# A three-layer feature-interaction network on one core: a new order of the set-up, folded weights made on TensorE, pooling inside the last chunk

## The chip, the cores and the metric

One core of a Trainium2 chip. The time is the device time of a whole run in microseconds (us); medians of several runs are given, with the lowest and highest where it matters. Positions in a trace are us from the start of the profiled span.

## The reference, cut to what matters

```python
# x: 1024 samples, F = 64 fields, E = 16 (1024, 64, 16); W0, W1, W2: 128 x 4096; fc_w: 1 x 256
h = x
for i in range(3):
    z = einsum('bfe,bge->bfge', x, h)              # all products of fields
    y = einsum('oc,bce->boe', W[i], z) + b[i]      # 128 outputs
    if i < 2:
        x_i, h = y[:, :64], y[:, 64:]              # one half is pooled, the other goes on
    else:
        x_i = y
    xs.append(x_i)
out = concat(xs, axis=1).sum(axis=2) @ fc_w.T + fc_b   # 1024 x 1
```

Only a weighted sum of the pooled outputs is wanted, so fc can be multiplied into the weights ahead of time. With V0, V1, V2 = fc times the pooled rows of W0, W1, W2 (each 64 x 64), layers 1 and 2 become sums of h1 times something that is linear in products of x again: M = V2 folded into the lower half of W1 (64 x 64 x 64), and M1 = the contraction of M with the same products of x that give h1. So one pass over the products yields h1 (64 columns) and M1 (64 columns) side by side, 128 columns of weights in all.

## The kernel before: the parts that matter

The samples run in 32 chunks of 32 (512 columns). A chunk has four VectorE products of 128 x 2048 (four tiles of 512 each), 16 matmuls over them, and one more over a "diagonal" tile. The weights are `w_all`, 17 tiles of 128 columns: 0 to 63 for h1 (from W0), 64 to 127 for M1. M must be read skewed, so it is stored to DRAM and read back: the **detour**. M1 of the first chunk can't begin until it is over.

```python
# V2 on VectorE: W2 is weighed with fc and summed, four times, ahead of everything
def weigh(w, fc, out):
    nk, n = out.shape[-1], fc.shape[-1]
    w = w.rearrange("p (k c) -> p k c", c=n)
    nc.vector.tensor_tensor(w, w, fc.unsqueeze(1).to_broadcast([128, nk, n]), ALU.mult)
    nc.vector.tensor_reduce(out, w, AX.X, ALU.add)

for k in range(4):
    cols = slice(k % 2 * 1024, (k % 2 + 1) * 1024)
    weigh(w2s[k // 2][:, cols], fcr[:, 128:256], v2h[:, 8 * k : 8 * k + 8])
# ... v2h into v2t, then M: eight matmuls, copies to m_sb, and the stores
nc.scalar.dma_start(out=md[0:64, 0:32, :], in_=m_lo)
nc.sync.dma_start(out=md[0:64, 32:64, :], in_=m_hi)
nc.scalar.dma_start(out=md[0:64, 64:96, :], in_=m_lo)
nc.sync.dma_start(out=md[64:96, 32:64, :], in_=m_hi[0:32])
nc.scalar.dma_start(out=md[64:96, 0:32, :], in_=m_lo[0:32])
nc.sync.dma_start(out=md[64:96, 64:68, :], in_=m_lo[0:32, 0:4, :])
nc.sync.dma_start(out=md[64:68, 64:96, :], in_=m_lo[0:4])     # corner, overlaps the last
# ...
side_by_side(ph, 0, range(NT + 1))        # h1 of chunk 0, in two halves of the array
# ... ten skewed reads of md, V1's and V0's loads, chunk 1's load
nc.vector.tensor_tensor(w_all[:, 0:NT, 64:128], ms1, ms2, ALU.add)
side_by_side(pq, 1, range(NT))            # M1 of chunk 0
weigh(w1x, fcr[:, 64:128], v1h)           # V1; V0 likewise, inside chunk 2
for c in range(1, NCH + 1):               # ... full chunks, 128 columns
    ...
# pooling behind the last chunk: 2 x 4 matmuls over acc, two activations, the output
```

## Time and profile before

| Part of the span | from (us) | to | length |
|---|---|---|---|
| V2 on VectorE, until M's matmuls start | 0 | 17.26 | 17.3 |
| M's matmuls and copies | 17.26 | 23.98 | 6.7 |
| stores of M | 23.98 | 36.2 | 12.2 |
| skewed reads, addition | 36.2 | 46.10 | 9.9 |
| M1 of chunk 0 to the last full-width matmul | 46.10 | 527.66 | 481.6 |
| behind it | 527.66 | 536.1 | 8.4 |

The median of the first three runs was 539.54 us (538.16 to 539.59). The chain of waits, the costliest groups and three stretches are shown in the prediction. Here is the timeline's line for the start of M1 (start, length, engine, line, operation, and the idle time ahead of it with what ended it):

```profile
46.10 8.42 PE L239 MATMUL pq<-z,w_all 128*64 128x256 f32 x64 [9.14 <-DVE w_all L280]
```

TensorE had been idle for 9.14 us when the addition that completes M1's weights released it.

### The profile page before, as it was taken

The numbers are of one execution on the slowest core, as the hardware profiler recorded it, in microseconds if no ns is written. First come the engines' busy times: TensorE is split into PE (matmuls) and PEld (weight loads), VectorE is DVE, ScalarE is ACT, GpSimd is POOL, SyncE is SP. The second block draws the span as 40 slices with busy tenths as digits, with TensorE's granted clock in tenths as the row PEclk, the third lists the DMA queues.
The fourth block names the chain that finished last, engine by engine and source line by source line (L and its number), as shares of the span: only waits on it lengthen the run. The fifth ranks groups of instructions, "written<-read, shape, count | busy, mean of one in ns | idle before, by whom it ended". The sixth has DMA issues, their size and how long they took to land.

```text
span 536.1 us, 3189 instructions
## 1 busy us (share of the span) xinstructions
PE 496.6 (93%) x1262; PEld 222.0 (41%) x1262; DVE 362.1 (68%) x222; ACT 79.1 (15%) x135; POOL 5.7 (1%) x18
## 2 busy tenths in 40 slices
PE   0465996999999999999999999999999999999997
PEld 0243442444444444444444444444444444444442
DVE  4654968687776767687776767687776767677822
ACT  0010110011111111011111111011111111101111
POOL 4000000000000000000000000000000000000000
PEclk9987998999999999999999999999999999999999
DMA  8669924433241434343341434434341424430000
GB/s 280 232 176 352 378 90 157 156 156 158 103 160 59 159 147 156 156 158 156 107 171 46 167 137 156 156 158 156 123 167 51 166 120 156 158 156 0 0 1 0
DMA packets 14152, 77.00 MB, mean 144 GB/s; under 512 B 3861, under 2 KB 4533, under 8 KB 5302
## 3 DMA queue, kind: packets, MB, share of 16 engines
q1 hardware_dynamic: 12058, 74.82, 36.2%
q10 hardware_dynamic: 1792, 1.98, 1.5%
q8 instruction: 10, 0.16, 0.1%
q0 software_dynamic: 288, 0.00, 0.0%
q14 instruction: 4, 0.03, 0.0%
HBM read 74.63 MB, written 2.17 MB: 143 GB/s over the span
## 4 chain that ended last, share of the span: by engine, by line
PE 89%; DMA 6%; DVE 3%; issue 0%; ACTq 0%; SPq 0%; ACT 0%; DVEq 0%
PE acc L191 80%; PE acc L205 5%; PE y L222 2%; DMA md<-m_sb 2%; DMA xb<-in_xrb 2%; DMA fcr<-in_fc_w 1%; PE pm L153 1%; DVE v2h L133 1%; DVE w L132 1%; DMA ms<-md 1%; DVE z L182 1%; PE po L354 0%; DVE uu L226 0%; DVE acc L227 0%; ACTq L271 0%
## 5 line engine op out<-in xcount | busy, mean ns | idle before, releaser
L191 PE MATMUL acc<-z,w_all 128*128 128x512 f32 x992 | 432.8, 594 | 4.7 <-DVE z L182 4.7
L191 PEld LDWEIGHTS acc<-z,w_all 128*128 128x128 f32 x992 | 188.9, 191 | 243.4 <-issue 230.0
L182 DVE TENSOR_TENSOR z<-xa,xb 128x2048 f32<-128x2048 f32 x128 | 284.5, 2281 | 1.6 <-DMA xb<-in_xrb 1.5
L214 DVE SCALAR_TENSOR_TENSOR uu<-acc,bh,q 64x512 f32<-64x512 f32 x31 | 23.1, 744 | 138.0 <-ACT q L213 138.0
L213 ACT COPY q<-acc 64x512 f32<-64x512 f32 x31 | 18.0, 582 | 398.6 <-PE acc L205 398.6
L205 PE MATMUL acc<-zl,w_all 128*128 128x512 f32 x62 | 31.7, 592 | 0.0
L153 PE MATMUL pm<-w1s,v2t 64*64 64x512 f32 x16 | 5.9, 863 | 17.3 <-DVE v2t L143 17.3
L196 ACT ACTIVATE zl<-xa 64x512 f32<-64x512 f32 x32 | 20.1, 629 | 5.6 <-DVE w_all L170 5.2
L227 DVE TENSOR_REDUCE acc<-uu 128x64 f32<-128x1024 f32 x16 | 19.5, 1220 | 0.5
L197 ACT COPY zl<-xa 64x512 f32<-64x512 f32 x32 | 19.7, 615 | 0.4
L201 ACT COPY xx<-xa 64x512 f32<-64x512 f32 x32 | 19.6, 614 | 0.4
L205 PEld LDWEIGHTS acc<-zl,w_all 128*128 128x128 f32 x62 | 11.8, 190 | 14.8 <-issue 14.8
L239 PE MATMUL pq<-z,w_all 128*64 128x256 f32 x64 | 8.4, 429 | 9.1 <-DVE w_all L280 9.1
L222 PE MATMUL y<-xx,bd 128*128 128x512 f32 x32 | 16.3, 592 | 0.0
L226 DVE SCALAR_TENSOR_TENSOR uu<-y,cx,xx 128x512 f32<-128x512 f32 x16 | 12.0, 751 | 4.8 <-PE y L222 4.3
L239 PE MATMUL ph<-z,w_all 128*64 128x256 f32 x64 | 8.8, 444 | 4.5 <-DVE w_all L170 4.5
L153 PEld LDWEIGHTS pm<-w1s,v2t 64*64 64x64 f32 x16 | 2.9, 196 | 19.4 <-DVE v2t L143 17.3
L239 PEld LDWEIGHTS pq<-z,w_all 128*64 128x64 f32 x64 | 5.0, 157 | 12.5 <-DVE w_all L280 9.6
L132 DVE TENSOR_TENSOR w<-w,fcr 128x1024 f32<-128x1024 f32 x4 | 4.9, 1217 | 7.2 <-DMA fcr<-in_fc_w 7.2
L222 PEld LDWEIGHTS y<-xx,bd 128*128 128x128 f32 x32 | 6.1, 190 | 7.7 <-issue 7.7
L239 PEld LDWEIGHTS ph<-z,w_all 128*64 128x64 f32 x64 | 5.3, 160 | 8.5 <-DVE w_all L170 5.4
L279 DVE MEMSET ms<- 64x64 f32 x1 | 0.1, 112 | 7.5 <-DMA ms<-md 7.5
(46 smaller groups left out, 39.2 us busy)
## 6 DMA issues: line engine op xcount, KB each, us to landing
xa<-in_xra SPq DMA_DIRECT2D x32, 1024.0 KB, 4.8
xb<-in_xrb SPq DMA_DIRECT2D x32, 1024.0 KB, 6.9
w<-in_wv SPq DMA_DIRECT2D x4, 512.0 KB, 7.3
w1s<-in_w1h SPq DMA_DIRECT2D x1, 1024.0 KB, 10.4
md<-m_sb ACTq DMA_DIRECT2D x2, 512.0 KB, 7.0
w1x<-in_wx SPq DMA_DIRECT2D x1, 1024.0 KB
w0x<-in_wx SPq DMA_DIRECT2D x1, 1024.0 KB, 12.5
w0t<-in_w0a SPq DMA_DIRECT2D x1, 544.0 KB
```

The costliest lines, as they stand in the source:

```text
L153: nc.tensor.matmul(pm[to], v2t[to], w1s[to, cols], start=True, stop=True)
L182: nc.vector.tensor_tensor(z, xas[c], xbs[c][:, j, :].unsqueeze(1).to_broadcast([128, NI, N]), ALU.mult)
L191: nc.tensor.matmul(accs[c], w_all[:, t, :], z[:, i, :], start=(t == 0), stop=False)
L196: nc.scalar.activation(zl[0:64], xas[c][0:64, 0, :], AF.Square)
L197: nc.scalar.copy(zl[64:128], xas[c][64:128, 0, :])
L201: nc.scalar.copy(xxs[c // 2][to], xas[c][to, 0, :])
L205: nc.tensor.matmul(accs[c], w_all[:, NT, :], zls[c], start=False, stop=True)
L213: nc.scalar.copy(q, accs[c][64:128])
L214: nc.vector.scalar_tensor_tensor(uus[c // 2][to, 0, :], accs[c][0:64], bh1[0:64], q, ALU.add, ALU.mult)
L222: nc.tensor.matmul(ys[k], bd, xxs[k], start=True, stop=True)
L227: nc.vector.tensor_reduce(acc[:, :, k, :], uus[k].rearrange("p k (b e) -> p k b e", e=E), AX.X, ALU.add)
L239: nc.tensor.matmul(p[halves[n]], w_all[:, t, cols], z[:, n * H2 : (n + 1) * H2], start=(t == 0), stop=(t == NT),)
```

## The change

Its intent: TensorE should have work while M makes its detour, and V0 to V2 should not cost VectorE's time. Loads of x and W0 come first; the h1 halves of three chunks (not one) run ahead of M1; V2 and later V0, V1 are made by TensorE, with fc as a weight of 32 equal columns in four quarters of the array, and spread by small SBUF-to-SBUF DMAs; 15 of the 16 pairs of chunks are pooled inside the last chunk.

```diff
+    x_tiles(0)
+    load_xa(0)
+    load_xb(0, slice(0, 1))                                # x first, xb and W0 in pieces
+    nc.sync.dma_start(out=w0s[:, 0:NI], in_=w0p[:, 0:NI])
+    load_xb(0, slice(1, NJ))
+    nc.sync.dma_start(out=w0s[:, NI:NT], in_=w0p[:, NI:NT])
+    for k in range(2):
+        nc.sync.dma_start(out=w2s[k], in_=wv2[:, k * 2048 : (k + 1) * 2048])
+    nc.sync.dma_start(out=w1s, in_=w1h)
+    load_chunk(1)
     ...
+    product(0, 0)
+    h1_weights(slice(0, NI))
+    side_by_side(0, 0, group(0))
     ...                                                    # groups 1, 2 likewise
+    load_chunk(2)
-    for k in range(4):
-        weigh(w2s[k // 2][:, cols], fcr[:, 128:256], v2h[:, 8 * k : 8 * k + 8])
+    for n in range(2):
+        pv = ps.tile([128, 512], F32, tag="set", name=f"pv2_{n}")
+        for k in range(4):
+            nc.tensor.matmul(pv[32 * k : 32 * k + 32], fv2, w2s[n][:, k * 512 : (k + 1) * 512],
+                             start=True, stop=True, tile_position=(0, 32 * k))
+        nc.scalar.copy(v2r[:, n, :], pv)
+        for to in halves:
+            nc.scalar.dma_start(out=v2t[to.start + 32 * n : to.start + 32 * n + 32],
+                                in_=v2r[0:128:32, n, :].rearrange("k (o f) -> k o f", f=F))
     ...                                                    # M's matmuls; four copies on ScalarE
-    nc.sync.dma_start(out=md[0:64, 32:64, :], in_=m_hi)
-    nc.scalar.dma_start(out=md[0:64, 64:96, :], in_=m_lo)
+    nc.scalar.dma_start(out=md[0:64, 32:64, :], in_=m_hi)
+    nc.sync.dma_start(out=md[0:64, 64:96, :], in_=m_lo)
-    nc.sync.dma_start(out=md[64:68, 64:96, :], in_=m_lo[0:4])
+    nc.sync.dma_start(out=md[64:68, 68:96, :], in_=m_lo[0:4, 4:32, :])
+    for c in (1, 2):                                       # h1 of chunks 1, 2 in the detour
+        last_tile(c)
+        for j in range(NJ):
+            product(c, j)
+            side_by_side(c, 0, group(j))
+        side_by_side(c, 0, [NT])
     ...                                                    # reads, addition
+    for k in range(2):                                     # the upper rows of W0, W1
+        nc.sync.dma_start(out=w01s[k], in_=w01[:, k * 2048 : (k + 1) * 2048])
     ...                                                    # V0, V1 as V2; M1 of chunks 0 to 2
+            if c == NCH - 1:
+                pool(first, 1)                             # 15 pairs, inside the last chunk
+                pool(first, 0)
```

(`for c in (1, 2)` stands for two written-out blocks.)

## The prediction

> **What bounds the kernel now.** I read the page's rows by busy time first, then the chain of waits, then stretches of the first 90 us and the order of events in them. The costliest groups (busy us, mean ns of one, idle before):
>
> ```profile
> L191 PE MATMUL acc<-z,w_all 128*128 128x512 f32 x992 | 432.8, 594 | 4.7 <-DVE z L182 4.7
> L182 DVE TENSOR_TENSOR z<-xa,xb 128x2048 f32<-128x2048 f32 x128 | 284.5, 2281 | 1.6 <-DMA xb<-in_xrb 1.5
> ```
>
> 31 of the 32 chunks use 16 tiles each and each fp32 matmul leaves two records: 31 x 16 x 2 = 992. TensorE is busy 93% of the span, VectorE 68%. The chain, in order of time (start, us, what):
>
> ```profile
> 0.75 6.40 DMA fcr<-in_fc_w
> ...
> 17.26 5.93 PE pm L153 x16
> ...
> 25.17 8.63 DMA md<-m_sb
> ...
> 33.86 2.33 DMA md<-m_sb
> ...
> 37.81 4.62 DMA ms<-md
> ...
> 83.89 2.29 DVE z L182
> ...
> 107.93 13.73 PE acc L191 x32
> 121.66 0.86 PE acc L205 x2
> ...
> 527.69 0.59 ACT q L213
> ...
> 531.14 1.90 PE po L354 x8
> ```
>
> From 107.93 on a chunk costs 13.73 + 0.86 = 14.59 us with no gap, so 0.858 us for one matmul of 512 columns, plus 0.86 for V0x once in a pair of chunks. VectorE needs 4 x 2.28 + 0.74 + (0.75 + 1.22)/2 = 10.9 us a chunk and follows. The steady part can't shrink; only what surrounds it can: about 56 us ahead of the first full chunk, a hole near 82 to 86, and 8.4 us behind the last V0x matmul. Stretches (PE, PEld, DVE, ACT, POOL busy, then clock, DMA share, GB/s):
>
> ```profile
> 38.00:40.00 2.00, 0.00 (x0) 0.00 (x0) 0.00 (x0) 0.00 (x0) 0.00 (x0) 1.00 1.01 246
> 82.00:84.00 2.00, 0.00 (x0) 0.00 (x0) 1.97 (x3) 0.00 (x0) 0.00 (x0) 1.00 0.02 4
> 86.00:88.00 2.00, 1.78 (x2) 0.79 (x3) 2.00 (x2) 0.00 (x0) 0.00 (x0) 0.58 0.46 127
> ```
>
> TensorE has nothing to do while M travels to memory and back, and nothing at 82, where VectorE weighs W0 ahead of the products; after the hole the clock is 0.58.
>
> **What the Trainium skill says.** "TensorE: Matmul & The Clock Gate", Part 1: after an idle window of about 3.4 us the array falls to half clock and needs a busy window to recover. The trace agrees: TensorE idled 4.5 us before the first h1 contraction, whose clock was 0.57 in 28 to 30 us and 1.00 from 32 on. "TensorEngine Tiling (Array Packing)", Key Properties: tiles of the array work independently. It agrees for two column halves: M1's 16 tiles (64 records of 256 columns) took 8.42 us from cold; alone they would need 64 x 0.215 = 13.8 us at full clock, side by side 6.85. Four quarters appear in no row yet. "DMA: Bandwidth & Descriptors", Queues, rings and completion order: an engine takes turns between queues by packet, so a small transfer still waits behind a full queue. The 16 KB copy of M's diagonal took 5.3 us to land beside the chunk loads, which agrees.
>
> **The change part by part.**
>
> 1. *Start.* V2 first (four weighings and sums on VectorE, 17.26 us until M's matmuls could start) becomes x and W0 first. Needed for the first product: 1 MB xa + 0.25 MB xb; then 0.25 MB of W0. Data starts to flow at about 2 us; the stretches read 37 to 199 GB/s until 6 us, when the broadcast read of fc (128 rows of the same 1 KB, landed 7.15) ends, and 383 to 434 GB/s from then on. I take that coincidence as the cause, and the change drops that read, so I reckon with 0.41 MB/us from 2.0: x at 5.1, W0's piece at 5.8. Product 5.4 to 7.7, weights 0.3 (a quarter of 1.23), TensorE starts at 8.0. Four tiles cold at 2 x 0.427 = 0.853 us: 11.4. Rest of W0 added (three quarters of 1.23 = 0.92) by 11.4, third product at 13.8, so three groups are through at about 15.7.
> 2. *V2 on TensorE.* Two rounds of four matmuls in quarters, 0.86 us a round if they run together: 1.7 us, to 17.5 (W2 has landed: 5 MB, 14.2). Then ScalarE in order: copy 0.59, two DMA issues at about 0.55, copy 0.59, two issues: the last is issued at about 19.7. Landing beside a full load queue 4.5 to 5.3 (rows above): v2t at 24.5. This takes the place of VectorE's 17.26: M's matmuls start 7 us later than before.
> 3. *M.* Group 3 and the diagonal end at 19.5; TensorE idles 5 us and is cold, so M's 16 records cost 5.9 as before: 30.3. ScalarE's last copy 0.6. The stores took from 23.98 to 34.35 (the third on ScalarE's queue, issued 25.85 + 8.5 landing) and then the overlapping corner 2.33 more; the change cuts the overlap, so 10.4: 41.3. The skewed reads took 8.6 (36.2 to 44.8), the addition 1.23: M1 can begin at **51.2**, against 46.1.
> 4. *Filling the detour.* Chunks 1 and 2's h1 halves, 2 x 17 x 0.43 = 14.6 us of TensorE, run between 30 and 46. VectorE makes their 8 products from 21.5 (8 MB landed) to about 40, so they are in time. About 5 us stay idle, and the restart is cold.
> 5. *From M1 on, on TensorE alone:* cold restart 1.6 (8.42 - 6.85); M1 of three chunks 3 x 6.85 = 20.6; three diagonals 1.3; V0 and V1 1.7; constants 0.45; 29 chunks x 14.59 = 423.1; 16 V0x x 0.858 = 13.7; pooling of 15 pairs inside the last chunk, two matmuls of 480 columns, 2 x 0.80 = 1.6. Sum 464.1. Before, the same stretch is 527.66 - 46.10 = 481.6. The gain of 17.5 is the two h1 halves (14.6) and the hole at 82 with its cold restart (4.3 + about 2), less V0/V1 and pooling.
> 6. *Tail.* Behind the last matmul: q 0.59, factors 0.74, a sum of 64x512 (half of 1.22, 0.65), a matmul of 32 columns about 0.3, activation 0.25 (its 1x1 row), the output 2.35 (533.75 to 536.1), joints 0.2: 5.1, against 8.4.
>
> Sum: 51.2 + 464.1 + 5.1 = 520.4 us of span. The timed median lies 3.4 above the span of the profile before, its own profiled run 1.9 above; with 2.3 between them I predict **522.7 us**, 16.8 less, 3.1%.
>
> **Rivals.**
>
> (a) *V2's way through SBUF is short.* If the DMAs land in about 2.5 us, v2t is there at 22, TensorE idles under 3 us, stays at full clock and M's matmuls cost 3.5, not 5.9. M1 begins near 46.5: measured about 518. For it: the loads are in another queue and these pieces are 8 KB each. Against: no small transfer under load landed below 3 us in the trace before.
>
> (b) *The slow start stays*, because it belongs to the first microseconds of any run and not to the broadcast read. Then 1.25 MB is there only at 7.4, all of step 1 to 3 slips by 2.3, and the time is 525. For it: those packets of W2 moved slowly on their own queue; a later load (86.2) had no slow ramp, which speaks against.
>
> (c) *The four quarters run one after another.* V2 costs 6.9 instead of 1.7, and V0/V1 the same: 10 us, so 533, within 2%. Against: two halves did run together, and nothing ties the quarters. I give it 7%.
>
> (d) *VectorE or a buffer becomes the bound.* W01's second MB, chunks 3 and 4 queue behind the addition of M1, 5 MB: chunk 3 at 9.5 us after M1 begins, its products by 18.7, chunk 4's by 28, factors and V0x's product by 31. TensorE wants chunk 3 at 26.5, the next V0x at 33.4, chunk 4 at 41. The margins are 7.8, 2.7 and 13 us, so no stall, but the 2.7 is thin and worth at most a few us. With 13 product buffers later, VectorE's 10.9 against 14.59 leaves it ahead. V0 and V1's six DMAs must land while M1 of chunk 2 (6.85 us) runs: two copies, six issues, landing makes 7.5; a wait of 0 to 2 us.
>
> (e) *The gain is hidden anyway.* The share of busy time says no: TensorE is on the chain for 89% of the span, and each us taken from its stream shifts all behind it.
>
> **Range and chances.** Steps 5 and 6 rest on durations of the trace and may be off by 2 us together; the start of M1 carries the doubt, 46.5 to 54. That spans 517 to 526; stalls of (d) and measuring scatter widen it upward, so 516.5 to 529.5. The threshold for faster by 2% is 528.7, 6 us above my number: it takes (b) with stalls, or (c), to miss it. Chance of faster 0.85, same 0.14, slower 0.01.
>
> **What would show each step.** Start: the first h1 matmul near 8.0 (10.3 if the slow start stays), and DMA above 350 GB/s from 3 us. V2: its eight matmuls (16 records) in 1.7 to 2 us, 7 if they are serial. M's matmuls start at 24.5, 5.9 long and cold, with an idle TensorE of some 5 us ahead. M1 begins at 51, after an idle stretch of 5 us, not 9. From there no gap of TensorE above 1 us to the end, which comes 5.1 behind its last full matmul. I am wrong if TensorE waits for VectorE in chunks 3 to 5, if the second detour (V0, V1) stops it ahead of the diagonals, or if the steady chunk is no longer 14.59 us.

## The result, and the profile after

| | median (us) | lowest to highest | runs |
|---|---|---|---|
| before | 539.32 | 538.16 to 539.59 | 4 |
| after | 535.58 | 535.20 to 535.99 | 4 |

The ratio of after to before is 0.9935 (95% interval 0.9918 to 0.9952): faster by 0.65%, within 2%, and 12.9 us above the 522.7 predicted. Ratios here and below are the recorded ones, for the runs of the same rounds; they are not quite the ratios of the medians quoted. The profiled run of after took 535.20 us with a span of 533.4 at a mean granted clock of 0.982; before's took 537.95, 536.1 and 0.987.

The chain of waits of after, in order of time (start, us, what), answers to the chain in the prediction:

```profile
2.12 9.51 DMA xb<-in_xrb
...
15.18 5.67 PE acc L224 x32
20.85 1.04 PE pv L273 x8
...
22.53 1.12 ACTq L280
...
25.47 6.13 DMA v2t<-v2r
31.61 6.03 PE pm L296 x16
...
41.34 8.93 DMA md<-m_sb
...
51.70 4.56 DMA ms<-md
...
56.28 5.17 DMA ms<-md
...
61.84 1.24 DVE w_all L341
...
63.12 15.96 PE acc L224 x128
...
528.68 0.59 ACT q L194
...
530.82 0.23 PE po L402 x2
```

Up to 63.12 the chain is made of transfers, VectorE and a few short pieces of TensorE: M's way. From there it is TensorE without a gap. M1 begins at 63.12, where before had 46.10. That alone is 17.0 us lost. What was won lies behind it: from M1's start to the last full-width matmul 528.66 - 63.12 = 465.5 us against 481.6, a gain of 16.0; behind the last matmul 533.4 - 528.66 = 4.7 against 8.4, a gain of 3.7. 16.0 + 3.7 - 17.0 = 2.7, the difference of the two spans.

TensorE's waits in after (engine and line, what ended the wait: us in total, times, longest) name the same places:

```profile
PE acc L224 <- DVE w_all L245: 11.5, 2, 10.1
PE acc L224 <- DVE w_all L341: 10.7, 1, 10.7
PE pm L296 <- DMA v2t<-v2r: 6.6, 1, 6.6
```

The first is the start, the second the wait for M1's weights, the third the wait for V2's scatter. There is no wait for VectorE's products behind M1 and none for V0 and V1. The first two costly groups by busy time show why the rest went well (busy us, mean ns of one, idle before):

```profile
L167 PE MATMUL acc<-z,w_all 128*128 128x512 f32 x928 | 405.5, 592 | 0.0
L224 PE MATMUL acc<-z,w_all 128*64 128x256 f32 x384 | 48.6, 416 | 22.2 <-DVE w_all L245 11.5
```

29 chunks instead of 31 run at full width, never idle; three chunks run as halves of 64 columns. How V2 and its scatter (the four small DMAs that spread V2 into `v2t`) followed the first three groups (a group is the four tiles of one product) is in the timeline of after:

```profile
20.78 1.92 PE L273 MATMUL pv<-w,fv 128*32 128x512 f32 x16
21.91 0.59 ACT L278 COPY v2r<-pv 128x512 f32<-128x512 f32 x1 [14.37 <-PE pv L273]
22.53 1.71 ACTq L280 DMA_DIRECT2D v2t<-v2r  x2
24.28 0.59 ACT L278 COPY v2r<-pv 128x512 f32<-128x512 f32 x1 [1.78 <-DMA v2t<-v2r]
24.89 1.11 ACTq L280 DMA_DIRECT2D v2t<-v2r  x2
```

V2's 16 records took 1.92 us. One after another they would have taken 16 x 0.43 = 6.9, so the four quarters ran together. ScalarE then copied, issued two DMAs in 1.71 us, copied, and issued two more.

### The profile page after: what moved, and what is told of

It reads as the page before. It is cut to its first block, busy times and chain, and to the rows that moved or that the text cites. A ratio compares the mean times of both kernels' runs of the same rounds, so it can differ in the third digit from the quotient of the medians.

```text
span 533.4 us, 3675 instructions
## 1 busy us (share of the span) xinstructions
PE 500.3 (94%) x1490; PEld 228.2 (43%) x1490; DVE 341.4 (64%) x203; ACT 81.7 (15%) x141; POOL 7.0 (1%) x23
## 3 DMA queue, kind: packets, MB, share of 16 engines
q10 hardware_dynamic: 1964, 1.92, 1.7%
## 4 chain that ended last, share of the span: by engine, by line
PE 90%; DMA 6%; DVE 1%; SPq 1%; ACT 0%; ACTq 0%; issue 0%; DVEq 0%
PE acc L167 75%; PE acc L224 6%; PE acc L183 5%; PE y L201 3%; DMA ms<-md 2%; DMA xb<-in_xrb 2%; DMA md<-m_sb 2%; DMA v2t<-v2r 1%; PE pm L296 1%; DVE z L159 0%; ACTq L280 0%; PE po L402 0%; SPq L303 0%; PE pv L355 0%; DVE w_all L341 0%
## 5 line engine op out<-in xcount | busy, mean ns | idle before, releaser
L167 PE MATMUL acc<-z,w_all 128*128 128x512 f32 x928 | 405.5, 592 | 0.0
L167 PEld LDWEIGHTS acc<-z,w_all 128*128 128x128 f32 x928 | 176.2, 190 | 222.3 <-issue 216.3
L224 PE MATMUL acc<-z,w_all 128*64 128x256 f32 x384 | 48.6, 416 | 22.2 <-DVE w_all L245 11.5
L194 ACT COPY q<-acc 64x512 f32<-64x512 f32 x29 | 16.9, 582 | 341.8 <-PE acc L183 331.0
L195 DVE SCALAR_TENSOR_TENSOR uu<-acc,bh,q 64x512 f32<-64x512 f32 x29 | 21.6, 743 | 65.8 <-ACT q L194 65.4
L224 PEld LDWEIGHTS acc<-z,w_all 128*64 128x64 f32 x384 | 29.3, 150 | 41.2 <-DVE w_all L245 12.3
L183 PE MATMUL acc<-zl,w_all 128*128 128x512 f32 x58 | 29.6, 592 | 0.0
L208 DVE TENSOR_REDUCE acc<-uu 128x64 f32<-128x1024 f32 (+2 forms) x18 | 20.2, 1129 | 0.6
L340 DVE MEMSET ms<- 64x64 f32 x1 | 0.1, 112 | 12.3 <-DMA ms<-md 12.3
L360 ACT COPY v01r<-pv 128x512 f32<-128x512 f32 x2 | 1.2, 588 | 35.7 <-PE pv L355 33.8
L341 DVE TENSOR_TENSOR w_all<-ms 128x1024 f32<-128x1024 f32 x1 | 1.2, 1224 | 5.7 <-DMA ms<-md 5.7
```

Source lines behind the costliest of these rows:

```text
L167: nc.tensor.matmul(accs[c], w_all[:, t, :], zs[c, j][:, i, :], start=(t == 0), stop=False)
L183: nc.tensor.matmul(accs[c], w_all[:, NT, :], zls[c], start=False, stop=True)
L194: nc.scalar.copy(q, accs[c][64:128])
L195: nc.vector.scalar_tensor_tensor(uu, accs[c][0:64], bh1[0:64], q, ALU.add, ALU.mult)
L208: nc.vector.tensor_reduce(acc[rows, parts, k, :], uus[k][rows, parts].rearrange("p k (b e) -> p k b e", e=E), AX.X, ALU.add,)
L224: nc.tensor.matmul(accs[c][halves[n], part * H2 : (part + 1) * H2], w_all[:, t, cols], z[:, n * H2 : (n + 1) * H2], start=(t == 0), stop=( ...
```

## The experiments

The **theory** after reading the two traces: what the change does for TensorE works as planned, and it is given back because M's way (V2, M's matmuls, stores, reads) starts later and takes longer. Every us by which M1 begins earlier should come back nearly whole, down to the point where TensorE has no more h1 halves to fill the detour with. **Rivals**: filling the detour did not help (the h1 halves only moved), or the later part has hidden losses that an earlier M1 would not recover; and for each term of M's way, whether it is the load rate, the crowding by other transfers, or the operation itself. Fourteen kernels ran, numbered in the order of running and grouped here by question; "before" stands for the medians of the runs beside them, 538.89 (1 to 4), 539.27 (5 to 8), 539.77 (9 to 12) and 539.52 (13, 14). Differences to after are differences of medians from different rounds; the medians of before in those rounds lie within 0.9 us. Runs 1 to 4 were on one chip, 5 to 8 on a second, 9 to 14 on a third.

### 1. M's way first (e1_chain_first)

Only the order is changed: W2 and W1 load first, V2's matmuls and scatter come ahead of the products, chunk 0's h1 behind M's matmuls.

```diff
+    for k in range(2):
+        nc.sync.dma_start(out=w2s[k], in_=wv2[:, k * 2048 : (k + 1) * 2048])
+    nc.sync.dma_start(out=w1s, in_=w1h)
     x_tiles(0)
     load_xa(0)
     ...
-    for k in range(2):
-        nc.sync.dma_start(out=w2s[k], ...)
-    nc.sync.dma_start(out=w1s, in_=w1h)
     # V2's matmuls, copies, scatter: moved ahead of product(0, 0)
-    side_by_side(0, 0, group(0))        # groups 0 to 3 and the diagonal ...
     # M's matmuls, copies, stores
+    side_by_side(0, 0, range(NT + 1))   # ... moved here
```

> Only order is changed: W2 and W1 are loaded ahead of x and W0, and V2's eight matmuls and the way to v2t stand ahead of the products and of chunk 0's h1 half, which now runs after M's matmuls. Theory (the change lost its gain because x and W0 first put V2 and with it M's whole way to memory and back 14 us later): W2 lands near 9 to 10, M's matmuls start at 20 to 22 instead of 31.6, M1 begins at 51 to 53 instead of 63.1, all three h1 halves still fit ahead of it, and the time falls by the same 10 to 12 us, to 523 to 526. Rival (the detour cannot be used: VectorE's twelve products, 27 us, or the loads behind the weights set the start of M1): M's matmuls start early, but TensorE reaches M1 only after the h1 halves, near 60, with no idle stretch ahead of it, and the time stays within 4 us of 535.6.

Measured: 522.36 us (521.66 to 523.32), ratio 0.9687 (0.9662 to 0.9713). Its chain of waits:

```profile
1.93 7.24 DMA fc<-in_fc_w
...
11.09 1.98 PE pv L254 x8
...
16.05 2.89 DMA v2t<-v2r
19.08 6.52 PE pm L291 x16
...
33.49 8.64 DMA md<-m_sb
...
51.80 14.03 PE acc L224 x128
```

V2 waited for fc's own load of one value per partition, until 11.09, yet M's matmuls began at 19.08 instead of 31.61 and M1 at 51.80 instead of 63.12, 11.3 us earlier. The time fell by 13.2; 1.9 of the difference is that M1 of chunks 0 and 1 met a running array (14.03 us for its 128 records instead of 15.96, since the h1 halves ended at 51.7). With not one instruction of the change taken out, most of the predicted gain is there. The theory holds, and hidden losses behind M1 are ruled out.

### 2. V2's scatter without loads behind it (e2_loads_held)

The loads of chunks 1 and 2 are issued by ScalarE behind V2's scatters, so that no load of x is queued while the scatters are under way.

```diff
-    load_chunk(1)              # ahead of V2, on SyncE's queue
-    load_chunk(2)
     # V2's matmuls, copies and scatters
+    load_chunk(1, nc.scalar)
+    load_chunk(2, nc.scalar)
```

> The loads of chunks 1 and 2 are issued by ScalarE behind V2's four small DMAs instead of ahead of them. Theory (the 6.1 us to landing of v2t is queueing behind 4 MB of loads): landing falls to about 2.5 to 3.5, M's matmuls start at 28 to 29 instead of 31.6, M1 begins about 3 us earlier and the time is near 532.5. Rival (the landing is the latency of such a scatter of 64 pieces of 256 bytes, whatever else moves): M's matmuls start at 31 to 32 as before and the time is 535 to 537, with chunk 1's products later.

Measured: 528.88 us (528.38 to 529.85), ratio 0.9804 (0.9776 to 0.9832), 6.7 us below after. Two lines from its timeline, the second pair of scatters and M's matmuls:

```profile
23.42 1.10 ACTq L278 DMA_DIRECT2D v2t<-v2r  x2
25.24 4.18 PE L296 MATMUL pm<-w1s,v2t 64*64 64x512 f32 x16 [1.67 <-DMA v2t<-v2r]
```

The last scatter was issued at 23.99 (chain of waits), and M's matmuls began 1.25 us later; in after 6.13 passed between the same two. As a consequence TensorE was idle for only 1.67 us, not 6.6, and M's 16 records took 4.18 us instead of 6.03. The Trainium skill says in "TensorE: Matmul & The Clock Gate", Part 1, that an idle window of about 3.4 us puts the array at half clock. Traces agree: the granted clock was 0.50 from 30 to 32 us in after, where M's matmuls began, and 1.00 from 24 to 26 in this run. M1 began at 56.88, 6.2 us earlier than in after. That is more than the expected 3 us: the landing gave 4.9, M's matmuls and copies 1.9 for the clock, which I had not counted, and V2 began 1.4 earlier in this trace (as it did in run 8, whose edit lies behind it, so by chance), while the stores took 1.9 longer. It wasn't free: h1 of chunk 1 then waited 6.4 us for its x.

### 3. What the skewed reads compete with (e3_reads_quiet, e8_reads_alone, e12_stores_before)

In after the reads took 11.5 us (50.35 to 61.84), before 8.6. The suspect is a 1 MB load of W01 that is queued just then. The first try swapped the two W01 loads, so that the one whose buffer is free later would come first.

```diff
-    for k in range(2):
+    for k in (1, 0):
         nc.sync.dma_start(out=w01s[k], in_=w01[:, k * 2048 : (k + 1) * 2048])
```

> The two loads of W0 and W1's kept halves change places, so that both wait for the addition of M1 and none runs beside the skewed reads of M. Theory (the reads took 11.5 us instead of the 8.6 I assumed because a 1 MB load was issued among them at 56.0): reads take 8.6 to 9.5, M1 begins about 2 us earlier, time near 533.5. Rival (the reads are bound by issue, five per queue, and by their 64-partition pieces): no change beyond 0.5 us, 535 to 536.

Measured: 536.07 us, ratio 0.9935 (0.9909 to 0.9960), no change. The trace shows why it tells nothing: a 1 MB load was again issued at 55.72, beside the reads. (My reading of the program is that buffers are handed out in the order of writing, so that the load that is written first gets the free one.) The edit was empty.

The second try makes both loads wait: VectorE writes one column of each target, and this write stands behind the addition that the reads feed.

```diff
     w01s = [set_tile(f"w01_{k}") for k in range(2)]
+    for k in range(2):
+        nc.vector.memset(w01s[k][:, 0:1], 0.0)
     for k in range(2):
         nc.sync.dma_start(out=w01s[k], ...)
```

> The run with the two loads in changed places did not do what was meant: a 1 MB load was still issued at 55.7, among M's skewed reads. Here VectorE writes one column of both targets behind the addition of M1, so both loads really wait. Theory (that load makes the reads take 11.5 us): the last read lands about 3 us after its issue instead of 5.2, the reads take 9 to 9.5, M1 begins 2 us earlier, time near 533.5. Rival (issue and small pieces bind): reads stay at 11 to 11.6, time 535 to 536.5.

Measured: 531.21 us (530.81 to 532.88), ratio 0.9853 (0.9829 to 0.9878), 4.4 below after. In its profiled run, which happened to be the slowest of the four, the reads took from 51.02 to 59.01, 8.0 us where before had 8.6, and M1 began at 60.56 although M's matmuls had started where they did in after (31.59). The span fell by only 2.3 there; the medians say more than this one trace.

The third gives M's stores back the order, queues and overlapping corner of before, to see what the cut of the corner was worth.

```diff
-    nc.scalar.dma_start(out=md[0:64, 32:64, :], in_=m_hi)
-    nc.sync.dma_start(out=md[0:64, 64:96, :], in_=m_lo)
+    nc.sync.dma_start(out=md[0:64, 32:64, :], in_=m_hi)
+    nc.scalar.dma_start(out=md[0:64, 64:96, :], in_=m_lo)
     ...
-    nc.sync.dma_start(out=md[64:68, 68:96, :], in_=m_lo[0:4, 4:32, :])
+    nc.sync.dma_start(out=md[64:68, 64:96, :], in_=m_lo[0:4])
```

> M's seven stores as in the kernel before, corner overlap and queues included, all else changed. Theory of the prediction (the overlap costs 2.3 us): stores take 14 to 14.5 us instead of 12.1, time 537.5 to 538. Rival (the corner store was hidden behind the slow small stores that end together with it): stores take 12 to 12.6, time 535 to 536.

Measured: 531.13 us (531.12 to 532.26), ratio 0.9845 (0.9825 to 0.9865). Of the two expectations only the rival's length of the stores hit: they took 12.3 us (38.12 to 50.46), about as long as the 12.1 of after, so the cut of the corner had saved nothing. Its time, 535 to 536, did not: the kernel was 4.4 us faster. The timelines of after and then of this run, DMA issues near the reads (start, us, queue, line, what), show what happened:

```profile
51.08 5.78 ACTq L335 DMA_DIRECT2D ms<-md  x4
55.49 0.47 SPq L339 DMA_DIRECT2D w_all<-md  x1
56.00 7.45 SPq L346 DMA_DIRECT2D w<-in_w  x2
```

```profile
51.20 4.79 ACTq L335 DMA_DIRECT2D ms<-md  x4
55.97 0.47 SPq L339 DMA_DIRECT2D w_all<-md  x1
56.48 2.90 SPq L346 DMA_DIRECT2D w<-in_w  x2
```

ScalarE issues four small reads of M (64 KB each); by the chain the last of them waits for an earlier read to land. In after it is issued at 56.28 (chain above), 0.28 us behind SyncE's 1 MB load, and takes 5.17 us to land. In this run it is issued at 55.41, ahead of the load, and lands in 2.28. With the load held (run 8) it landed in 2.35. In runs 2, 3, 7 and 13 it was issued behind the load again, by 0.3 to 0.4 us, and took 5.04 to 5.31. So one small transfer on the wrong side of a large one costs some 3 us, and which side it falls on is decided by issue times that nobody planned. Where the corner's saving went can be read from the chains. Before, the corner's store waited for the store that it overlaps, was then issued at 33.86 into a quiet queue and took 2.33 us. In after it no longer waits: it is issued at 41.34, 3.1 us behind the first store, joins the crowd and takes 8.93 us. Both ways end 12.1 to 12.2 us behind the first store.

### 4. The slow start (e4, e5, e6, e11, e13)

The first product ran at 7.41 us (predicted 5.4), the second waited for the rest of xb until 11.66. Two candidates: the loads of fc and biases, one value to a partition, which GpSimd issues in these microseconds; and the pieces of x and W0, whose rows are 2 to 6 KB instead of 8. And one question to the prediction: was before's slow start really fc's broadcast read?

**e4_bias_late** moves the eight bias loads behind the work that needs fc.

```diff
     nc.gpsimd.dma_start(out=fc01, in_=fc_w[0, 0:128].unsqueeze(1))
-    # eight bias loads on GpSimd's queue
     # memsets, fv2, fv01 (they wait for fc)
+    # the eight bias loads
```

> GpSimd's eight small bias loads are issued after fc's two have landed, so they are out of the first 8 us. Theory (the element-sized transfers slow the first loads: 193 to 277 GB/s between 5 and 10 us): over 350 GB/s from 3 us on, x's first piece lands at 5.5 to 6, TensorE starts 1.5 to 2 us earlier, time near 534. Rival (the first microseconds of loads are slow for another reason, or 2 KB rows are): rates of 5 to 10 us stay near 200, TensorE's first matmul stays at 10.1, time 535 to 536.

Measured: 535.43 us, ratio 0.9925 (0.9896 to 0.9954). In the stretch 8 to 10 us the rate rose to 405 GB/s from 234, but from 4 to 8 it stayed low (181, 207), the rest of xb landed only 0.6 us earlier (11.04), and the time stayed.

**e5_small_after_x** issues every small load, fc's too, only when x has landed.

```diff
+    nc.gpsimd.tensor_copy(fc2, xbs[0][:, NJ - 1, 0:1])    # waits for the last piece of x
     nc.gpsimd.dma_start(out=fc2, ...)                     # and all small loads behind it
```

> All of GpSimd's element-sized loads, fc's too, wait until x's last piece of chunk 0 has landed. Theory (those small loads, fc's included, slow the first 10 us; the run with only the biases held back still had fc's in it): over 350 GB/s from 3 us on, the first product starts at 5.5 to 6 instead of 7.4, TensorE at 8 to 8.5 instead of 10.1; fc lands near 17 and V2 may then wait for it, so the time gains less, 533 to 535. Rival (slow for another reason): the first product stays at 7.2 to 7.8, the rates stay near 200 between 5 and 9 us, and V2 waits for fc besides: 536 to 538.

Measured: 535.66 us, ratio 0.9929 (0.9905 to 0.9953). From 4 to 8 us still 247 and 213 GB/s; the first product at 7.47. fc now landed at 20.4 and V2 began at 22.19, which takes back what the rest may have won.

**e11_whole_rows** loads xb and W0 of chunk 0 whole, in rows of 8 KB, the small loads left where they were.

```diff
-    load_xb(0, slice(0, 1))
-    nc.sync.dma_start(out=w0s[:, 0:NI], in_=w0p[:, 0:NI])
-    load_xb(0, slice(1, NJ))
-    nc.sync.dma_start(out=w0s[:, NI:NT], in_=w0p[:, NI:NT])
+    load_xb(0, slice(0, NJ))
+    nc.sync.dma_start(out=w0s, in_=w0p)
```

> The changed kernel with xb and W0 of chunk 0 loaded whole, in rows of 8 KB, not in a first quarter of 2 KB rows and a rest of 6 KB rows. Theory (short rows are why the loads move at 143 to 250 GB/s between 5 and 8 us, with small loads held back too): above 330 GB/s from 3 to 8 us, both of x's pieces there by 8, all of W0 by 10.7; the first product starts at 7.9 to 8.3, the second follows without a wait, V2's matmuls start near 18 to 18.5 instead of 20.8, time 533 to 534. Rival (slow start for another reason): rates under 280 at 5 to 8 us, first product at 9 or later, time 535.5 to 538.

Measured: 534.42 us, ratio 0.9897 (0.9877 to 0.9916): 320, 246 and 254 GB/s from 4 to 10, x complete at 10.24. Not the cure either.

**e13_whole_and_small_late** does both, the edits of 5 and 11 together, as one look.

> The changed kernel with chunk 0's xb and W0 loaded whole and all element-sized loads held until x has landed. If short rows and small loads together are the slow start: above 340 GB/s from 3 to 10 us, 2.1 MB there by 8, the first product at 7.9 to 8.3. If a third cause is left: rates below 280 somewhere between 5 and 9 us, first product at 9 or later. The total says little here, since V2 has to wait for fc.

Measured: 534.81 us in a single run. Stretches of after, then of this run (PE, PEld, DVE, ACT, POOL busy, then clock, DMA share, GB/s):

```profile
4.00:6.00 2.00, 0.00 (x0) 0.00 (x0) 0.00 (x0) 0.35 (x1) 1.64 (x4) 1.00 0.78 275
6.00:8.00 2.00, 0.00 (x0) 0.00 (x0) 0.59 (x1) 1.51 (x3) 0.22 (x1) 1.00 0.81 221
8.00:10.00 2.00, 0.00 (x0) 0.00 (x0) 2.00 (x2) 0.00 (x0) 1.79 (x9) 1.00 0.69 234
```

```profile
4.00:6.00 2.00, 0.00 (x0) 0.00 (x0) 0.00 (x0) 0.23 (x1) 0.00 (x0) 1.00 0.96 377
6.00:8.00 2.00, 0.00 (x0) 0.00 (x0) 0.00 (x0) 1.63 (x3) 0.00 (x0) 1.00 1.06 446
8.00:10.00 2.00, 0.00 (x0) 0.00 (x0) 1.70 (x1) 0.00 (x0) 1.44 (x4) 1.00 0.99 412
```

Now the rate is what I had reckoned with, 377 to 446 GB/s. Short rows and one-value loads slow the start together; taking away one of them leaves much of it. Whole rows are also fewer transfers, and no run separates the two. TensorE's first matmul came only at 11.25, as it waited for the whole of W0, but V2 began at 19.17, 1.6 us ahead of after. Still M's matmuls began only 0.6 us earlier, at 30.97. Set side by side, the starts of V2's and M's matmuls (timelines, us) show why no edit of the start moved the time:

| run | V2 | M | loads of chunks 1 and 2 |
|---|---|---|---|
| 13 | 19.17 | 30.97 | ahead of the scatter |
| 8 | 19.29 | 31.59 | ahead |
| 4 | 20.28 | 31.48 | ahead |
| after | 20.78 | 31.59 | ahead |
| 11 | 21.59 | 30.40 | ahead |
| 5 | 22.19 | 31.82 | ahead |
| 2 | 19.34 | 25.24 | behind |
| 14 | 20.66 | 26.57 | behind |

(In the other four runs with the loads ahead, V2 began at 20.51 to 20.89 and M at 31.97 to 32.35.) With the loads queued ahead, M's start does not follow V2's; it comes as the loads run out (in after 420 GB/s from 28 to 29 us, 314 to 30, 71 to 31, 0 to 32). With the loads behind, M follows V2 by 5.9 us both times. So in this order it was the queued loads that set M's start, and an earlier V2 only waited longer. (In run 1 the scatter landed in 2.89 us at 360 GB/s, so it is not the rate as such. I take it to be the amount that is queued ahead; no run varies that alone.)

**e6_before_fc_rows** asks the question to the prediction: before, with fc's broadcast read replaced by 128 different rows (of W0; the result is wrong).

```diff
-        out=fcr, in_=bass.AP(tensor=fc_w.tensor, offset=0, ap=[[0, 128], [1, 256]])
+        out=fcr, in_=w0b[:, 0:4, :].rearrange("p t g -> p (t g)")
```

> The kernel before, but its broadcast read of fc (128 times the same 1 KB) is replaced by 128 different rows of 1 KB of W0, so the result is wrong on purpose. Theory of the prediction (the broadcast read made the loads slow until 6 us): above 350 GB/s from 3 us on, V2's first weighing starts at 3.5 to 4.5 instead of 7.17, time 2 to 3 us shorter. Rival (the start is slow in any case): rates of 140 to 200 GB/s until 6 us and the first weighing at 6 to 7.2, time within 1 us.

Measured: 538.59 us in a single run beside 539.27 for before. The first weighing began at 6.16 instead of 7.17, M1 at 44.95 instead of 46.10; from 2 to 4 us the rate was still 195 GB/s (150 in before), from 4 to 6 it was 299 (177 in before). So the broadcast read had taken part of the rate and cost V2's start about 1 us, but without it the first weighing came far behind the 3.5 to 4.5 that would bear out the prediction. What else slows before's first 4 us was not tested.

### 5. Whether filling the detour is worth anything (e7_no_fill, e9_no_fill2)

The rival that the h1 halves of chunks 1 and 2 only moved. The first try put their matmuls behind the loads of chunks 3 and 4 in the program.

```diff
-        side_by_side(1, 0, group(j))        # chunks 1 and 2, in the detour
     ...
     load_chunk(4)
+    for c in range(1, 3):
+        side_by_side(c, 0, range(NT + 1))
     side_by_side(0, 1, range(NT))
```

> The changed kernel with the h1 halves of chunks 1 and 2 put behind M1's weights instead of into the detour; all else stays. Theory (the filling works in full, and its 14.6 us were given back by the later chain): TensorE idles during the whole detour, M1's weights are ready at 62 to 63 as before, and the time rises by 14 to 16.5 us (the restart stays cold), to 550 to 552. Rival (the filling brought little, since TensorE had to wait for M1 anyway): the time rises by less than 5 us.

Measured: 535.31 us, ratio 0.9920 (0.9894 to 0.9947). Empty again: between the old place and the new one stands nothing on TensorE, so the matmuls ran where they had run, from 38 to 52 us. The second try puts them behind `side_by_side(0, 1, range(NT))`, the M1 half of chunk 0.

> The run meant to leave the detour unfilled did not: nothing on TensorE stood between, so the same matmuls ran in the same place. Here the h1 halves of chunks 1 and 2 stand behind chunk 0's M1 half in TensorE's order, so they cannot start before M1's weights. Theory (the filling works in full, 14.6 us, and was given back by the later chain): TensorE idles from about 45 to 63, M1 begins at 62 to 63.5 as before, and the time rises by 14 to 15 us to 549 to 551. Rival (filling is worth little): rise below 5 us.

Measured: 549.10 us (548.44 to 549.92), ratio 1.0172 (1.0154 to 1.0189). Stretches of after and then of this run:

```profile
38.00:52.00 14.00, 14.00 (x132) 9.34 (x130) 5.79 (x3) 3.87 (x7) 0.00 (x0) 1.00 0.69 157
52.00:64.00 12.00, 1.33 (x10) 0.53 (x6) 1.34 (x2) 0.00 (x0) 0.00 (x0) 0.70 0.69 174
```

```profile
38.00:52.00 14.00, 0.00 (x0) 0.00 (x0) 6.41 (x3) 4.08 (x7) 0.00 (x0) 0.67 0.67 154
52.00:64.00 12.00, 0.42 (x2) 0.30 (x4) 1.34 (x2) 0.00 (x0) 0.00 (x0) 0.50 0.73 176
```

TensorE does nothing in the detour, M1 starts where it did in after (63.58), and the time is 13.5 us longer: the 14.6 us of two h1 halves, nearly whole. Filling works; the rival falls. Without it the change would have been a loss of 1.7%.

### 6. Together (e14_held_and_alone, e10_best)

**e14** joins the edits of runs 2 and 8 and leaves the order of the change alone.

> The changed kernel, x and W0 still first, with chunks 1 and 2's loads behind V2's small DMAs and with W0 and W1's kept halves behind the addition of M1. If the two costs are separate: M1 begins 2 to 3 us before the 56.9 that holding the loads gave alone, near 54, and the time is 525 to 527, within the range predicted for the change itself. If they overlap, or if TensorE's h1 halves (ending at 53.6 there) are the next bound: M1 near 56, time 527.5 to 529.

Measured: 526.93 us (526.37 to 527.26), ratio 0.9762 (0.9745 to 0.9779), 8.7 below after, where 6.7 and 4.4 would add to 11.1. M's matmuls were warm (4.19 us), the reads took 45.59 to 52.7, M1 began at 55.44. The missing 2.4 us are not settled: h1 of chunk 2 ended only at 54.97, so that nothing could have brought M1 forward by more than 0.5 us; the addition waited its last 1.44 us for the small read of M's diagonal, and further on the chain runs through products of VectorE (76.85 to 88), which in after it does not, though TensorE idled only 0.52 us for them.

**e10** starts from run 1, holds the W01 loads as run 8, loads fc by ScalarE at the very start, puts the biases late and gives x a third buffer (smaller pools pay for it).

```diff
-    xp = ctx.enter_context(tc.tile_pool(name="xp", bufs=2))
+    xp = ctx.enter_context(tc.tile_pool(name="xp", bufs=3))
-    nc.gpsimd.dma_start(out=fc2, in_=fc_w[0, 128:256].unsqueeze(1))
+    nc.scalar.dma_start(out=fc2, in_=fc_w[0, 128:256].unsqueeze(1))
     load_chunk(1)
+    load_chunk(2)
     ...                                   # biases behind fv2, fv01
+    for k in range(2):
+        nc.vector.memset(w01s[k][:, 0:1], 0.0)
```

> Chain first, plus: the loads of W0 and W1's kept halves behind the addition of M1, fc loaded by ScalarE's queue and the biases late, a third buffer for x so that chunk 2 loads without a wait (smaller pools elsewhere make the room). If the start of M1 is what all of this moves: V2's matmuls start at 8 to 9.5 instead of 11.1, the stores have no load beside them and take 10 to 12 us instead of 16, M1 begins near 47 instead of 51.8, time 517 to 519. Rival (once the chain is short, VectorE's twelve products and TensorE's h1 halves set the start of M1): M1's weights are ready before TensorE is, and the time stays at 519.5 to 522.

Measured: 519.39 us (517.62 to 520.68), ratio 0.9618 (0.9593 to 0.9644). Its chain of waits:

```profile
0.74 6.15 DMA fc<-in_fc_w
...
7.21 1.98 PE pv L255 x8
...
12.19 6.30 DMA v2t<-v2r
...
37.57 4.86 DMA ms<-md
...
47.42 14.04 PE acc L225 x128
```

M1 begins at 47.42, near the 47 expected, and 0.7 us behind the end of the last h1 half, so TensorE hardly waits for M's way any more. The time is a little above the 517 to 519 expected with it. This version beats both kernels: 3.8% below before, 16.2 us below after.

## Why the prediction was wrong

It said 522.7 us, 516.5 to 529.5, and faster by over 2% with a chance of 0.85. The time was 535.58, outside the range, and within 2%. Its span of 520.4 was 13.0 short of 533.4. Steps 4, 5 and 6 hold; steps 1 to 3, the start of M1 ("M1 can begin at 51.2"), failed and carry 11.9 of the 13.0. What failed in them is above all the landing of small transfers: M's matmuls were to start at 24.5 and started at 31.6, as V2's scatter landed behind the loads of chunks 1 and 2, and M's reads took 11.5 us instead of 8.6, as the last of them fell behind a 1 MB load.

| Step, as predicted | predicted | measured | off by |
|---|---|---|---|
| 1: three groups through | 15.7 | 20.78 | +5.1 |
| 2: V2's matmuls to the last scatter issued | 4.0 | 4.7 | +0.7 |
| 2: landing | 4.8 | 6.13 | +1.3 |
| 3: M's matmuls and last copy | 6.5 | 6.7 | +0.2 |
| 3: stores | 10.4 | 12.1 | +1.7 |
| 3: reads | 8.6 | 11.5 | +2.9 |
| **M1 begins** | 51.2 | 63.12 | **+11.9** |
| 5: from there to the last full-width matmul | 464.1 | 465.5 | +1.4 |
| 6: tail | 5.1 | 4.7 | -0.4 |

The table follows the chain of one trace; its rows are not independent gains, as step 1 shows.

- *Step 1.* Three things were wrong. "I reckon with 0.41 MB/us from 2.0" took a coincidence as the cause; the measured rates were 275, 221 and 234 GB/s from 4 to 10 us, and runs 5, 11 and 13 show that short rows (or the number of pieces) and one-value loads together cause them, run 6 that the broadcast read had cost before's V2 about 1 us. This puts the first product at 7.41 instead of 5.4, near the 2.3 us of rival (b). And I overlooked a wait: the second product needs the rest of xb, queued behind W0's first piece, which came at 11.66. Then groups 1 and 2 took 5.67 us, where one group took 1.95 in run 8; that trace, with the same program up to there, had V2 begin at 19.29, so 1.5 us of the 5.1 are scatter. And in no run did an earlier V2 help by itself: with the loads queued, M's start did not follow V2's (table in section 4).
- *Step 2.* The quarters ran together (1.92 us against 1.7), so rival (c) falls. The landing was longer than the 4.5 to 5.3 that I took from the trace before, as it fell among the 1 MB loads of chunks 1 and 2; runs 2 and 14 show 1.25 us without them. The page that the prediction cites states only that an engine takes turns between queues; that a small transfer waits behind a full queue was my inference, and it held, but its length was set by what was queued and not by a fixed landing. In runs 8 and 13, where V2 began 1.5 to 1.6 us earlier than in after, the scatter only waited longer. What rival (a) hoped for is possible, not with these loads ahead.
- *Step 3.* M's matmuls cost 6.03, cold, as said. The 2.33 us that the corner's cut was to save came to nothing (run 12), and the reads met a 1 MB load (runs 8 and 12), which I had no term for: I copied the 8.6 us from before, where the next 1 MB load was issued at 41.51, just behind the last read (41.3).
- *Step 4.* The two h1 halves ran in the detour from 37.6 to 52.4. Run 9 puts their worth at 13.5 us. TensorE's idle ahead of M1 was 10.7, not 5, as M's way was longer.
- *Steps 5 and 6.* Right to 1.4 and 0.4 us. A steady chunk remained 13.73 + 0.86; the hole at 82 is gone; neither V0, V1 nor the buffers stopped TensorE, so rival (d) falls.
- *Rival (e)*, the gain is hidden anyway, was dismissed with the share of busy time. It is the wrong view for the first 60 us, in which the end is set by M's way and not by TensorE: there each us of M's way counted, and the change put 17.0 us on it, where the prediction had allowed 5.1.

The range was too narrow for the same reason. It allowed the start of M1 46.5 to 54 us, though that number was a sum of ten terms under crowded queues, most of them taken from another order of transfers. Run 1 ends at 522.36 us, near the predicted time, only because the same parts stand in an order that the prediction had not been asked about.

## What to carry to other kernels

When a set-up has one long chain of small dependent transfers, start that chain before everything, and fill the time with movable work; the same instructions in two orders differed by 13.2 us here. Hold large loads until the small transfers that others wait for are issued, and predict a landing only from a row with the same traffic around it. Before you read a result of a reordering, look in the trace whether the order changed at all: two of these edits (runs 3 and 7) were empty.

## What the Trainium skill lacked or had wrong

- "DMA: Bandwidth & Descriptors" states in Specifications that 512 B is the least transfer for line rate. The runs show less than line rate with rows of 2 KB and up while loads of one value to a partition are under way: 221 to 275 GB/s from 4 to 10 us in after, 377 to 446 when both were changed (run 13); 213 to 247 from 4 to 8 us with rows of 2 to 6 KB alone (run 5). The page has no figure for what such small loads take from large ones in other queues.
- The same page has no figure for how far the landing of a small transfer grows under queued loads: 1.25 us (run 2) against 6.13 (after) for V2's last scatter, and 2.28 (run 12) against 5.17 (after) for one read of M that was issued just ahead of or just behind a 1 MB load.
- "TensorEngine Tiling (Array Packing)" gives only a theoretical speedup for four column tiles (up to 4, in Theoretical Speedup), and the measured table of "TensorE: Matmul & The Clock Gate", Part 3, has three column tiles (2.38) and not four. Measured for fp32 and 512 columns: 16 records in 1.92 us, against 6.9 estimated one after another, a factor of 3.6.
- I found no page with a case in which one of several reads was issued only when an earlier one had landed, so that the order of transfers on different queues shifted: ScalarE's four issues of reads took 5.78 us in after and 4.79 in run 12, and this decided whether the last one went ahead of the load. Whether the chip or a wait that the program was given holds the issue, no run here shows.
